# A two-layer convolution block on one core: the last image's depthwise filter is spread over more engines and its gate is placed later

## The chip, the cores and the metric

The kernel runs on one core of one Trainium2 chip. The core has five engines that run their own instruction streams in order and meet through semaphores: TensorE (PE; its weight loads are shown apart as PEld), VectorE (DVE), ScalarE (ACT), GpSimd (POOL) and SyncE (SP), which here only issues DMAs. The metric is the device time in microseconds (us) of one execution. Before the change three runs took 3316.29, 3316.36 and 3316.74 us; their median is 3316.36.

## The reference

Eight images of 384 channels and 64 x 64 points pass two residual layers. The first normalises over groups of channels, projects to queries, keys and values (1x1 convolutions), turns queries and keys by a rotary embedding, and applies linear attention in six heads. The second is the one that matters here:

```python
# layer 1, on the group-normalised x; hid = 384, P = 8
t = einsum('bchw,oc->bohw', x, w_in)                 # 1x1 expansion
tf = rfft2(t in patches of 8 x 8) * fft_filter        # filter in the frequency domain
t = irfft2(tf)                                        # back to points
t = conv3x3(t, w_dw, feature_group_count=hid)         # depthwise: 9 taps for each channel
x1, x2 = t[:, :192], t[:, 192:]
x = x + einsum('bchw,oc->bohw', gelu(x1) * x2, w_out) # gate, contraction, residual
```

Everything is 32-bit floating point.

## The kernel before

An image is cut into 8 bands of 8 rows (512 points), and its 384 channels into three tiles of 128 partitions. The channels of layer 1 are permuted so that tile 0 holds the first 128 channels of `x1`, tile 1 their partners of `x2`, and tile 2 the remaining 64 of each, in its lower and upper 64 partitions.

Layer 1 of a band runs through these steps; the names are those of the code and the trace:

1. `normalised` (L374, ACT): three instructions write `hf`, the normalised band, one band ahead.
2. `expand_filter` (L746): 12 matmuls `pi` (L752, PE), each shown as two records, give the expansion in four PSUM tiles; ACT copies each to `ht` (L759). Then 8 matmuls `pd` (L766) transform it, and four VectorE multiplies `tf` (L774) apply the frequency filter.
3. `back_transform` (L777): 48 small matmuls `pb` (L787) go back to points; six ACT copies (L797) lay the band, with a border, into one of two buffers, `ring`, which serve bands in turn. Two more ACT copies exchange border rows with the neighbour band: L802 gives this band its upper border row, L803 gives the band before its lower one. Until L803 has run, the band before lacks the row for its last three taps.
4. `first_taps` (L840): for each tile ACT writes the first of the nine taps into `dw`, in SBUF (L844). `taps` (L857): the other eight follow as VectorE instructions `acc = ring * w + acc` (L855), 24 for a band. They run one band late.
5. `gate_taps` (L863): ACT's gelu of the first part (L867) and a VectorE multiply by the second (L868) into `gated`, and the same for the two halves of tile 2 (L871, L872). There is one `gated` tile.
6. `contraction` (L878): 12 matmuls `pw` (L888 and L899) from `gated` into four PSUM tiles; ACT copies them into `y` (L913), and GpSimd's queue issues a DMA that adds `y` to the output in memory (L918), where the residual was stored before. For the very last band VectorE adds the residual itself (L915) and SP stores (L916).

For all images but the last this layer is interleaved with the key and value projections of the next image, so that TensorE always has other work. The last image has none. In its last two bands the taps of tile 2 are therefore matmuls with diagonal matrices (L822, tile `ptap`), nine for a band, on diagonals that `make_diagonals` (L813) writes once with nine ACT instructions.

PSUM has eight tiles, given out by one pool. The order of instructions on each engine is made by a scheduler when the program is built: it follows the order of the source as priority, but moves an instruction ahead of others that it expects to wait. The loop of the last image is written in the order expansion, store, normalisation of the next band, back transform, first taps, contraction of the band two before, taps and gate of the band before.

Of the kernel before, what the change touches and what calls it, by code (L numbers as in the profile page):

```python
# [9 lines left out]
F32 = mybir.dt.float32  # L10
BF16 = mybir.dt.bfloat16
AF = mybir.ActivationFunctionType
ALU = mybir.AluOpType

P = 128
C = 384
CT = 3
H = W = 64
N = H * W
NBAND = 8  # L20
BT = N // NBAND
# [96 lines left out]
def conv_blocks_kernel(ctx: ExitStack, tc: tile.TileContext, a: dict, out: bass.AP, nb: int):  # L118
    nc = tc.nc
# [4 lines left out]
    taps_pool = ctx.enter_context(tc.tile_pool(name="taps", bufs=2))  # L124
    qp = ctx.enter_context(tc.tile_pool(name="qp", bufs=2))
    small = ctx.enter_context(tc.tile_pool(name="small", bufs=2))
# [3 lines left out]
    def ps_tile(name):  # L130
        return psum.tile([P, 512], F32, tag="ps", name=name)

    def w_tile(shape, name):
        return work.tile(shape, F32, tag="w", name=name)
# [13 lines left out]
    def store_x(b, j):  # L148

        if (b, j) != (nb - 1, NBAND - 1):  # L150
            nc.sync.dma_start(x_out[b][:, :, j * BT : (j + 1) * BT], xt.pop((b, j)))
# [81 lines left out]
    def const_tile(shape, name, src, queue=nc.scalar):  # L233
        t = const.tile(shape, F32, tag=name, name=name)
        queue.dma_start(t, src)
        return t
# [8 lines left out]
    ident = groups[:, 2 * CT * NG :]  # L245
# [5 lines left out]
    scale = HD ** -0.5  # L251
# [9 lines left out]
    ring = []  # L261
# [283 lines left out]
    latest = {}  # L545
# [200 lines left out]
    def expand_filter(b, j, h, done):  # L746
        ht = w_tile([P, 4, C], f"ht_{b}_{j}")
        tf = w_tile([P, 4, C], f"tf_{b}_{j}")
        for i in range(4):
            p_ = ps_tile(f"pi_{b}_{j}_{i}")  # L750
            for t in range(CT):
                nc.tensor.matmul(  # L752
                    p_[:, :C],
                    h[:, t, i * P : (i + 1) * P],
                    w_in[:, t, :],
                    start=(t == 0),
                    stop=(t == CT - 1),
                )
            nc.scalar.copy(ht[:, i, :], p_[:, :C])  # L759
        yield  # L760

        for s in range(2):
            p_ = [ps_tile(f"pd_{b}_{j}_{2 * s + i}") for i in range(2)]
            for above in range(2):
                for i in range(2):
                    nc.tensor.matmul(  # L766
                        p_[i][halves[above], :C],
                        dft[halves[i], :],
                        ht[halves[i], 2 * s + above, :],
                        start=True,  # L770
                        stop=True,
                    )
            for i in range(2):
                nc.vector.tensor_mul(tf[:, 2 * s + i, :], p_[i][:, :C], filt)  # L774
        done.append(tf)

    def back_transform(b, j, tf):  # L777
        t = ring[j % 2]
        for m0, m1 in ((0, 2), (2, 3)):


            ps = [ps_tile(f"pb_{b}_{j}_{m0}_{u}").rearrange("p (m s i n) -> p m s i n", m=2, s=2, i=2) for u in range(2)]
            for m in range(m0, m1):
                for k in range(4):
                    for c in range(2):
                        for u, half in enumerate(halves):
                            nc.tensor.matmul(  # L787
                                ps[u][halves[c], m - m0, k // 2, k % 2],
                                tf[half, k, m * P + 64 * c : m * P + 64 * c + 64],
                                idft[half, :],  # L790
                                start=True,
                                stop=True,
                            )
            for m in range(m0, m1):
                rows = t[:, m, 1:9, 1 : W + 1].rearrange("p r (s u i c) -> p u r s i c", s=2, u=2, i=2)
                for u in range(2):
                    nc.scalar.copy(rows[:, u], ps[u][:, m - m0].rearrange("p s i (r c) -> p r s i c", r=8))  # L797
        if j == 0:
            nc.gpsimd.memset(t[:, :, 0, :], 0.0)
        else:  # L800
            before = ring[(j - 1) % 2]
            nc.scalar.copy(t[:, :, 0, :], before[:, :, 8, :])  # L802
            nc.scalar.copy(before[:, :, 9, :], t[:, :, 1, :])  # L803
        if j == NBAND - 1:
            nc.gpsimd.memset(t[:, :, 9, :], 0.0)

    dw, dw_pe, diagonals = {}, {}, []

    def on_array(b, j):

        return b == nb - 1 and j >= NBAND - 2

    def make_diagonals():  # L813
        t = small.tile([P, CT, C], F32, tag="wk", name="diagonals", bufs=1).rearrange("p t c -> p (t c)")
        for k in range(9):
            nc.scalar.activation(t[:, k * P : (k + 1) * P], ident, AF.Copy, scale=w_dw[:, 2, k : k + 1])
        diagonals.append(t)

    def array_taps(b, j, ks):

        for k in ks:
            nc.tensor.matmul(  # L822
                dw_pe[b, j].rearrange("p (r w) -> p r w", w=W),
                diagonals[0][:, k * P : (k + 1) * P],
                ring[j % 2][:, 2, k // 3 : k // 3 + 8, k % 3 : k % 3 + W],
                start=(k == 0),
                stop=(k == 8),
            )

    first_on_vector = {}  # L830

# [8 lines left out]
    def first_taps(b, j):  # L840

        acc = dw[b, j] = taps_pool.tile([P, CT, 8, W], F32, tag="dw", name=f"dw_{b}_{j}")
        for m in range(CT - on_array(b, j)):
            nc.scalar.activation(acc[:, m], ring[j % 2][:, m, 0:8, 0:W], AF.Copy, scale=w_dw[:, m, 0:1])  # L844
        if on_array(b, j):
            dw_pe[b, j] = ps_tile(f"ptap_{b}_{j}")
            array_taps(b, j, range(9 if j == NBAND - 1 else 6))

    def tile_taps(b, j, m, weights, ks=None):

        t, acc = ring[j % 2], dw[b, j]
        for k in ks or range(first_on_vector.pop((b, j, m), 1), 9):
            src = t[:, m, k // 3 : k // 3 + 8, k % 3 : k % 3 + W]
            wd = weights[:, m, k : k + 1]
            nc.vector.scalar_tensor_tensor(acc[:, m], src, wd, acc[:, m], ALU.mult, ALU.add)  # L855

    def taps(b, j):  # L857
        if on_array(b, j) and j < NBAND - 1:
            array_taps(b, j, range(6, 9))
        for m in range(CT - on_array(b, j)):  # L860
            tile_taps(b, j, m, w_dw)

    def gate_taps(b, j):  # L863
        g = gated
        af = dw.pop((b, j)).rearrange("p t r w -> p t (r w)")
        last = dw_pe.pop((b, j)) if on_array(b, j) else af[:, 2, :]
        nc.scalar.activation(g[:, :BT], af[:, 0, :], AF.Gelu)  # L867
        nc.vector.tensor_mul(g[:, :BT], g[:, :BT], af[:, 1, :])  # L868
        for h, gelu in enumerate((gelu2[64:P, :], g[64:P, BT:])):
            of = slice(h * HT, (h + 1) * HT)  # L870
            nc.scalar.activation(gelu, last[0:64, of], AF.Gelu)  # L871
            nc.vector.tensor_mul(g[halves[h], BT:], gelu, last[64:P, of])  # L872

    def depthwise_gate(b, j):
        taps(b, j)
        gate_taps(b, j)
# [43 lines left out]
    def contract(b, j):  # L920
        run(contraction(b, j))
# [29 lines left out]
    def run(*chains):  # L951

        chains = list(chains)
        while chains:
            chains = [c for c in chains if next(c, chains) is not chains]
# [139 lines left out]
    for c0, at, n in QRUNS:  # L1095

        t, p0, quarter, first = at // P, at % P, c0 // QC, c0 % QC
# [13 lines left out]
    w_dw = const_tile([P, CT, 9], "w_dw", a["w_dw"], nc.sync)  # L1111
# [55 lines left out]
    before_last, late = nothing, iter(())  # L1167
    for b in range(nb):
# [4 lines left out]
        last = b == nb - 1  # L1173
# [14 lines left out]
        for j in range(NBAND):  # L1188
# [4 lines left out]
            tf = []  # L1193
            h = normalised(b, j, params, (8, 8), "f") if j else ahead
            store_x(b, j)
            if 1 <= j < NBAND - 1:
                load_x(b + 1, j + 1)
            layer1 = expand_filter(b, j, h, tf)
            items = 1 if j < 2 else 2

# [7 lines left out]
            some(2 * items)  # L1208
            back_transform(b, j, tf[0])
            first_taps(b, j)  # L1210
            some(items)
            if j > 1:
# [11 lines left out]
        late = last_band(b)  # L1224


    make_diagonals()
    b = nb - 1
    h = ahead
    for j in range(NBAND):  # L1230
        tf = []
        layer1 = expand_filter(b, j, h, tf)
        run(layer1)
        store_x(b, j)
        if j < NBAND - 1:
            h = normalised(b, j + 1, params, (8, 8), "f")
        back_transform(b, j, tf[0])
        first_taps(b, j)
        if j >= 2:
            contract(b, j - 2)  # L1240
        if j >= 1:
            taps(b, j - 1)
            gate_taps(b, j - 1)
    contract(b, NBAND - 2)
    taps(b, NBAND - 1)
    gate_taps(b, NBAND - 1)
    contract(b, NBAND - 1)


# [39 lines left out]
```

## Time and profile before

| what | us |
|---|---|
| median of three runs | 3316.36 |
| the profiled execution, its own time | 3317.55 |
| its span, first to last instruction | 3315.8 |
| TensorE busy in the span | 3256.2 |
| VectorE busy | 2755.8 |
| ScalarE busy | 2020.4 |
| GpSimd busy | 173.7 |
| last image's layer 1, from its first `pi` (3136.58) to the end of the span | 179.2 |

Times inside the profile are counted from the start of the span. A group's line names the source line, the engine, the operation, what it writes and reads, its shape and count; then its busy time, the mean of one in ns, and the idle time of the engine just before such instructions with what ended it. A timeline row gives start and length, merged over instructions that follow each other, and in brackets the idle time before it. In a table of stretches each engine's busy time stands with its number of instructions, and then the mean clock granted to TensorE, where 1.00 is full speed.

### The profile page before, as it was taken

What the parts mean: (1) busy time and instruction counts of PE and PEld (TensorE: products, weight loads), DVE (VectorE), ACT (ScalarE), POOL (GpSimd) and SP (SyncE); (2) the same over time, 40 slices, a digit from 0 to 9 for tenths busy, and PEclk for the clock granted to TensorE, in tenths of its full rate; (3) what the DMA queues carried; (4) which work ended last, traced back from release to release, by engine and by line L of the source; (5) the groups of instructions that cost most, each with busy time, mean ns of one, the idle gap of its engine ahead of it and who ended that gap; (6) DMA issues with size and microseconds to landing.
All of it is one profiled execution on the core that took longest, in us unless ns stands there. A gap on an engine that the chain in (4) does not pass through costs nothing.

```text
span 3315.8 us, 53150 instructions
## 1 busy us (share of the span) xinstructions
PE 3256.2 (98%) x21133; PEld 1829.5 (55%) x21133; DVE 2755.8 (83%) x4528; ACT 2020.4 (61%) x4029; POOL 173.7 (5%) x321
## 2 busy tenths in 40 slices
PE   8999999999999999999999999999999999999988
PEld 5544666456664566545665456654566446664454
DVE  6577789978889688896889968998788987889697
ACT  4445666666766566755666656656576665556553
POOL 0000000100010000100001000010000100000000
PEclk9999999999999999999999999999999999999999
DMA  7324334462444523534335433445343551334112
GB/s 217 114 87 117 93 80 117 127 143 68 106 108 127 143 68 96 128 114 127 87 87 137 119 112 77 111 127 118 99 102 91 144 128 52 73 73 126 58 30 48
DMA packets 154446, 346.33 MB, mean 104 GB/s; under 512 B 29813, under 2 KB 41061, under 8 KB 146005
## 3 DMA queue, kind: packets, MB, share of 16 engines
q1 hardware_dynamic: 124500, 282.65, 27.0%
q0 software_dynamic: 29504, 60.06, 12.4%
q8 instruction: 166, 2.72, 0.3%
q14 instruction: 84, 0.68, 0.1%
q10 hardware_dynamic: 192, 0.21, 0.0%
HBM read 235.62 MB, written 99.93 MB: 101 GB/s over the span
## 4 chain that ended last, share of the span: by engine, by line
PE 90%; DVE 5%; ACT 3%; DMA 1%; issue 1%; SPq 0%; DVEq 0%; ACTq 0%
PE pf L734 15%; PE pk L491 14%; PE pi L752 14%; PE pv L507 13%; PE pq L655 13%; PE pw L888 5%; PE pb L787 3%; PE pw L899 3%; PE acc L523 3%; PE pd L766 3%; PE acc L536 2%; DVE dw L855 2%; PE pn L693 1%; ACT mt L570 1%; PE prb L717 1%
## 5 line engine op out<-in xcount | busy, mean ns | idle before, releaser
L855 DVE SCALAR_TENSOR_TENSOR dw<-ring,w_dw,dw 128x512 f32<-128x512 f32 x1401 | 977.5, 746 | 239.9 <-ACT ring L803 200.8
L491 PE MATMUL pk<-wk,x 128*128 128x384 f32 x1536 | 544.9, 496 | 0.0
L655 PE MATMUL pq<-x,wq 128*128 128x512 f32 x1152 | 521.5, 601 | 2.6 <-ACT mt L570 2.6
L752 PE MATMUL pi<-w_in,hf 128*128 128x384 f32 x1536 | 513.5, 491 | 1.3 <-ACT hf L374 1.3
L734 PE MATMUL pf<-qc,mt 128*128 128x512 f32 x1152 | 510.7, 597 | 0.0
L507 PE MATMUL pv<-wv,x 128*128 128x384 f32 x1344 | 470.0, 488 | 0.0
L491 PEld LDWEIGHTS pk<-wk,x 128*128 128x128 f32 x1536 | 283.5, 191 | 205.4 <-issue 32.5
L752 PEld LDWEIGHTS pi<-w_in,hf 128*128 128x128 f32 x1536 | 288.1, 190 | 195.8 <-issue 2.5
L514 ACT COPY v<-pv 128x384 f32<-128x384 f32 x224 | 108.7, 485 | 424.5 <-PE pv L507 423.2
L734 PEld LDWEIGHTS pf<-qc,mt 128*128 128x128 f32 x1152 | 214.3, 190 | 255.5 <-issue 239.6
L507 PEld LDWEIGHTS pv<-wv,x 128*128 128x128 f32 x1344 | 253.6, 190 | 181.4 <-issue 8.4
L655 PEld LDWEIGHTS pq<-x,wq 128*128 128x128 f32 x1152 | 212.8, 190 | 250.6 <-issue 226.2
L738 DVE SCALAR_TENSOR_TENSOR x<-pf,bfc,x 128x512 f32<-128x512 f32 x192 | 138.6, 744 | 81.9 <-PE pf L734 81.4
L379 ACT ACTIVATE qs<-qc 128x512 f32<-128x512 f32 (+1 forms) x128 | 107.0, 836 | 144.2 <-DVE qc L684 143.8
L180 ACT ACTIVATE differences<-x,shift 128x512 f32<-128x512 f32 x168 | 120.0, 714 | 103.8 <-DVE x L738 103.6
L888 PE MATMUL pw<-gated,w_out 128*128 128x256 f32 x768 | 179.3, 383 | 0.0
L494 DVE TENSOR_TENSOR kc<-pk,kvbias 128x384 f32<-128x384 f32 x256 | 140.7, 550 | 40.3 <-PE pk L491 40.2
L759 ACT COPY ht<-pi 128x384 f32<-128x384 f32 x256 | 115.1, 482 | 85.6 <-PE pi L752 81.8
L888 PEld LDWEIGHTS pw<-gated,w_out 128*128 128x128 f32 x768 | 146.7, 192 | 36.9 <-issue 6.9
L918 POOL DMA_DIRECT2D out_dram<-y x63 | 80.5, 1277 | 1544.6 <-DVE dw L855 799.1
L379 ACT ACTIVATE ks<-kc 128x1536 f32<-128x1536 f32 x64 | 95.0, 1485 | 95.1 <-DVE kc L498 94.8
L374 ACT ACTIVATE hf<-x,nb,rs 128x512 f32<-128x512 f32 x192 | 146.4, 808 | 2.4 <-DVE nb L319 2.3
(209 smaller groups left out, 4375.1 us busy)
## 6 DMA issues: line engine op xcount, KB each, us to landing
tq<-in_tq SPq DMA_DIRECT2D x64, 1024.0 KB, 4.9
x<-in_x SPq DMA_DIRECT2D x64, 768.0 KB, 6.1
tk<-in_tk SPq DMA_DIRECT2D x64, 768.0 KB, 4.5
out_dram<-x SPq DMA_DIRECT2D x63, 768.0 KB, 3.7
out_dram<-y POOLq DMA_DIRECT2D x63, 768.0 KB, 7.7
xs<-in_x SPq DMA_DIRECT2D x56, 768.0 KB, 5.9
dw<-tap POOLq DMA_DIRECT2D x14, 512.0 KB, 9.3
wk<-in_wk SPq DMA_DIRECT2D x8, 576.0 KB, 3.9
```

Of the source, the lines that this page charges most:

```text
L180: nc.scalar.activation(out[:, m, :], x_[:, m, :], AF.Identity, bias=shift[:, m : m + 1], accum_out=of_m[0])
L374: nc.scalar.activation(dst, src, AF.Identity, bias=nb_[:, t : t + 1], scale=rs[:, t : t + 1])
L379: nc.scalar.activation(e, x_, AF.Relu, scale=-1.0)
L491: nc.tensor.matmul(pk[:, :C], tokens(t), wks[:, t, :], start=(t == 0), stop=(t == CT - 1))
L494: nc.vector.tensor_add(kc[:, i, :], pk[:, :C], bias)
L507: nc.tensor.matmul(pv[:, :C], xt[b, j][:, t, i * P : (i + 1) * P], wvs[:, t, :], start=(t == 0), stop=(t == CT - 1),)
L655: nc.tensor.matmul(p_, wqs[:, t, m * P : (m + 1) * P], xt[b, j][:, t, :], start=(t == 0), stop=(t == CT - 1),)
L734: nc.tensor.matmul(p_, mt[:, t, m * P : (m + 1) * P], q[:, t, :], start=(t == 0), stop=(t == CT - 1))
L738: latest["sum"] = nc.vector.scalar_tensor_tensor(xm, p_, bfc[:, m : m + 1], xm, ALU.add, ALU.add).ins
L752: nc.tensor.matmul(p_[:, :C], h[:, t, i * P : (i + 1) * P], w_in[:, t, :], start=(t == 0), stop=(t == CT - 1),)
L855: nc.vector.scalar_tensor_tensor(acc[:, m], src, wd, acc[:, m], ALU.mult, ALU.add)
L888: nc.tensor.matmul(p_[h][:, m - m0, :], w_out[:, 0, m * P : (m + 1) * P], gated[:, h * HT : (h + 1) * HT], start=(m == m0), stop=False,)
```

## The change

Only the last image's layer 1 is touched.

- The sums of tiles 0 and 1 are kept in PSUM tiles (`sums`), where ACT writes the first tap and VectorE adds the others. The sum of tile 2 stays in SBUF.
- Tile 2's taps of bands 0 to 5 leave VectorE: ACT writes the products of three taps (`products`), GpSimd those of two early ones, and GpSimd adds all eight to the sum (`apart_taps`). In band 6 tile 2, and in band 7 tiles 1 and 2, are done by matmuls with diagonals; a second set of diagonals is made, in the buffer of the query weights.
- The taps are split by the rows they read: taps 1 to 5 (`early_taps`) are written in the band's own iteration, taps 6 to 8 (`late`), which need the row from the band below, in the next one.
- The gate of a band is written two iterations later, behind the expansion's matmuls of that iteration; `issue_after` keeps its instructions on ACT behind the third `ht` copy. The contraction of that band now stands ahead of the back transform.

In the built program nothing moves ahead of the last image's layer 1, but for the nine new ACT instructions that make the second diagonals. GpSimd's queue gets one instruction of its own ahead of its first product, which reloads its library.

```diff
+            turned = nc.scalar.copy(ht[:, i, :], p_[:, :C])
+            if i == 2:
+                latest["turned"] = turned.ins
...
     def make_diagonals():
+        for m, tag in ((2, "wk"), (1, "wq")):
+            t = small.tile([P, CT, C], F32, tag=tag, name=f"diagonals_{m}", bufs=1).rearrange("p t c -> p (t c)")
+            for k in range(9):
+                nc.scalar.activation(t[:, k * P : (k + 1) * P], ident, AF.Copy, scale=w_dw[:, m, k : k + 1])
+            diagonals[m] = t
...
+    on_array = {NBAND - 2: (2,), NBAND - 1: (1, 2)}
+    def array_taps(j, m, ks):
+        for k in ks:
+            nc.tensor.matmul(
+                sums[j][m],
+                diagonals[m][:, k * P : (k + 1) * P],
+                ring[j % 2][:, m, k // 3 : k // 3 + 8, k % 3 : k % 3 + W],
+                start=(k == 0),
+                stop=(k == 8),
+            )
+    def apart_taps(j, m, ks):
+        products = w_tile([P, CT, 8, W], f"products_{j}_{ks[0]}")
+        for i, k in enumerate(ks):
+            if i == CT:
+                products = w_tile([P, CT, 8, W], f"products_{j}_{k}")
+            product = products[:, i % CT]
+            src = ring[j % 2][:, m, k // 3 : k // 3 + 8, k % 3 : k % 3 + W]
+            wd = w_dw[:, m, k : k + 1]
+            if i < CT:
+                nc.scalar.activation(product, src, AF.Copy, scale=wd)
+            else:
+                nc.gpsimd.tensor_scalar_mul(product, src, wd)
+            nc.gpsimd.tensor_add(sums[j][m], sums[j][m], product)
+    def early_taps(j):
+        on = on_array.get(j, ())
+        sums[j] = []
+        for m in range(CT):
+            if m < 2 or m in on:
+                t = ps_tile(f"sums_{j}_{m}").rearrange("p (r w) -> p r w", w=W)
+            else:
+                t = taps_pool.tile([P, CT, 8, W], F32, tag="dw", name=f"sums_{j}_{m}")[:, m]
+            sums[j].append(t)
+            if m not in on:
+                nc.scalar.activation(t, ring[j % 2][:, m, 0:8, 0:W], AF.Copy, scale=w_dw[:, m, 0:1])
+        more_taps(j, range(1, 6))
+    def more_taps(j, ks):
+        for m in reversed(range(CT)):
+            if m in on_array.get(j, ()):
+                array_taps(j, m, range(0 if ks[0] == 1 else ks[0], ks[-1] + 1))
+            elif m == 2:
+                apart_taps(j, m, ks)
+            else:
+                for k in ks:
+                    src = ring[j % 2][:, m, k // 3 : k // 3 + 8, k % 3 : k % 3 + W]
+                    t = sums[j][m]
+                    nc.vector.scalar_tensor_tensor(t, src, w_dw[:, m, k : k + 1], t, ALU.mult, ALU.add)
...
     make_diagonals()
     b = nb - 1
     h = ahead
+    late = range(6, 9)
     for j in range(NBAND):
         tf = []
         layer1 = expand_filter(b, j, h, tf)
+        next(layer1)
+        if j >= 2:
+            with tc.issue_after(latest["turned"]):
+                gate_sums(j - 2)
         run(layer1)
         store_x(b, j)
         if j < NBAND - 1:
             h = normalised(b, j + 1, params, (8, 8), "f")
-        back_transform(b, j, tf[0])
-        first_taps(b, j)
         if j >= 2:
             contract(b, j - 2)
-        if j >= 1:
-            taps(b, j - 1)
-            gate_taps(b, j - 1)
-    contract(b, NBAND - 2)
-    taps(b, NBAND - 1)
-    gate_taps(b, NBAND - 1)
-    contract(b, NBAND - 1)
+        back_transform(b, j, tf[0])
+        if j:
+            more_taps(j - 1, late)
+        early_taps(j)
+    more_taps(NBAND - 1, late)
+    for j in (NBAND - 2, NBAND - 1):
+        gate_sums(j)
+        contract(b, j)
```

In the order that the scheduler made of it, VectorE's stream of a middle band is: the six late taps of the band before, the ten early taps of this band, the three gate multiplies, the four `tf` multiplies of the next band; and TensorE's is `pi`, `pd`, `pw`, `pb`.

## The prediction

> **What bounds the kernel now.** The page of the profile first: TensorE is busy nearly the whole span, at full clock but for the ends, so over the whole kernel only matmuls count, and a faster VectorE is worth nothing there. The change touches only the last image's filter stage, so I read that stage alone, cut at the start of each band's expansion (PE L752).
>
> ```profile
> PE 3256.2 (98%) x21133; PEld 1829.5 (55%) x21133; DVE 2755.8 (83%) x4528; ACT 2020.4 (61%) x4029; POOL 173.7 (5%) x321
> L855 DVE SCALAR_TENSOR_TENSOR dw<-ring,w_dw,dw 128x512 f32<-128x512 f32 x1401 | 977.5, 746 | 239.9 <-ACT ring L803 200.8
> ```
>
> Stretches (columns: length, busy PE, PEld, DVE, ACT, POOL, clock, DMA share, GB/s):
>
> ```profile
> 3163.72:3181.97 18.25, 16.09 (x164) 10.18 (x161) 17.14 (x29) 14.75 (x34) 0.00 (x0) 1.00 0.00 1
> 3181.97:3202.81 20.84, 17.26 (x162) 11.17 (x160) 20.75 (x34) 10.10 (x25) 1.29 (x1) 0.92 0.26 39
> 3202.81:3222.54 19.73, 17.22 (x162) 11.46 (x161) 19.64 (x32) 12.03 (x28) 1.27 (x1) 0.91 0.28 42
> 3222.54:3242.77 20.23, 17.76 (x162) 11.14 (x160) 19.93 (x33) 10.09 (x25) 1.27 (x1) 0.92 0.27 40
> ...
> 3284.55:3307.19 22.64, 22.64 (x94) 14.15 (x95) 17.75 (x29) 7.13 (x16) 2.54 (x2) 1.00 0.27 38
> ```
>
> Bands 3 to 5 are bound by VectorE (20.75 of 20.84 us busy); TensorE has some 3 us to spare and runs part of each band at a lower clock; ScalarE is half idle and GpSimd nearly empty. The last rows are TensorE's alone. The timeline of one band gives durations and hops:
>
> ```profile
> 3210.75 1.52 PE L766 MATMUL pd<-ht,dft 64*64 64x384 f32 x16
> 3214.15 1.95 DVE L774 TENSOR_TENSOR tf<-pd,filt 128x384 f32<-128x384 f32 x4
> 3214.77 3.17 PE L787 MATMUL pb<-idft,tf 64*64 64x64 f32 x96 [2.50 <-DVE tf L774]
> 3217.56 1.78 ACT L797 COPY ring<-pb 128x256 f32<-128x256 f32 x6 [2.66 <-PE pb L787]
> 3219.17 0.41 ACT L802 COPY ring<-ring 128x198 f32<-128x198 f32 x1
> 3219.42 0.41 ACT L803 COPY ring<-ring 128x198 f32<-128x198 f32 x1
> 3219.68 1.99 ACT L844 ACTIVATE dw<-ring,w_dw 128x512 f32<-128x512 f32 x3
> ...
> 3299.04 2.75 PE L888 MATMUL pw<-gated,w_out 128*128 128x256 f32 x12
> 3301.72 1.57 PE L899 MATMUL pw<-gated,w_out 64*128 64x256 f32 x12
> 3303.23 2.86 PE L888 MATMUL pw<-gated,w_out 128*128 128x256 f32 x12
> ```
>
> Call R(j) the end of copy L803 in band j, when the taps of band j-1 can be finished: here 3219.83 for j=4. Read so, R(1) to R(7) stand at 3165.76, 3179.84, 3201.67, 3219.83, 3241.63, 3259.31, 3284.55. R(1) to R(6) take 93.5 us.
>
> **The change, part by part.**
>
> *Taps taken from VectorE.* 176 taps stood there (6 bands x 24, two x 16); 120 remain (7 x 16 + 8). A tap is issued every (12.01-0.747)/17 = 0.662 us, so 37 us leave VectorE. That is not the gain, as the next wait decides.
>
> *The gate's place; the sum.* In the new order VectorE runs, per band from 2 on: 6 late taps of band j-1, 10 early taps of band j, the gate of j-1, then the four tf multiplies of j+1. TensorE runs pi, pd, pw, then pb; before, pb followed tf and pw was slipped in around it. So a ring closes: the taps need R(j); the gate stands behind all 16; pw behind the gate; pb behind pw; the ring copies behind pb; and they make R(j+1). What waits behind each: on ScalarE the last ht copy and the next normalisation behind the gelus, on VectorE tf behind the gate, on TensorE pb behind pw. The copies of y, moved ahead of the ring copies on ScalarE, start 1.16 us after pw's second half (3294.86 to 3296.02), last 1.5, and are done at R+16.7, before pb's first copy at R+17.05. Its length: 16 x 0.662 = 10.6; gate multiply 0.69 and hop 0.05 (3302.49 + 0.69 to 3303.23); pw 2.68 + 1.49 = 4.17 (3299.04, 3301.72, 3303.2); pb of two tiles with its latency 1.5 (0.9 us for 48 of 64 records, 0.25 to the copy); copies 1.61 + 0.25 + 0.41 = 2.27; hops 0.02. Sum 19.3 us, against 93.5/5 = 18.7 now: VectorE is idle for some 5 us of it, and nothing is won. Only the first step wins: in band 1 tf waits for 10 taps instead of 12, as pd + 0.98 (band 0: 3146.29 to 3147.27) gives 3159.28 and the taps 3152.54 + 6.6 = 3159.2, against 3160.62: R(1) = 3164.45. R(6) = 3164.45 + 5 x 19.3 = 3260.95.
>
> *The clock.* The trace has half-clock spells of 3.41 us, each behind a stretch of the same length with little matmul work:
>
> ```profile
> 3211.87:3215.28 3.41, 0.90 (x24) 0.36 (x16) 3.32 (x8) 2.94 (x5) 0.00 (x0) 1.00 0.07 13
> 3215.28:3218.69 3.41, 3.41 (x86) 3.20 (x87) 3.41 (x7) 1.13 (x5) 0.00 (x0) 0.50 0.02 5
> 3232.35:3235.76 3.41, 1.29 (x48) 1.02 (x48) 3.38 (x7) 1.77 (x4) 0.00 (x0) 1.00 0.00 0
> 3235.76:3239.17 3.41, 3.41 (x60) 2.46 (x55) 3.35 (x7) 0.47 (x1) 0.00 (x0) 0.50 0.02 5
> ```
>
> In the new band pi ends at R+6.7, ht's last copy, behind nine ScalarE products and the gelus, at R+8.1, pd at R+9.05, and pw waits until R+11.35. On the same grid (194.80, 215.28, 235.76, 256.24 after 3000) the stretches before it hold about 0.9, 0.9, 1.15 and 1.2 us of matmuls for bands 3 to 6: all slow, as the rows above. pw then runs 3.1, 2.7, 2.55 and 2.45 us at half speed, losing half: 5.4 us in four bands. Band 2 (2.1 and 1.9 us of 3.41) I take as undisturbed. Bounds: 0 and 5 x 1.7 = 8.5. R(6) = 3266.35. The Trainium skill's "TensorE: Matmul & The Clock Gate" (Part 1) states a free-running window of about 3.4 us and half rate after an idle one. The trace agrees, and it speaks against this change; by a gate that opened at once the time would be the sum without 5.4.
>
> *Band 7 and the tail.* R(6) to R(7): six array taps 6 x 0.857 + 0.12 (nine took 7.83, 3284.35 to 3292.18, their weight loads 0.43 apart, two to a tap) from R-0.2, pi 7.94, pd 1.55, pw 4.17, pb and a bank 1.6, copies 2.27: 22.5, against 25.25 (there the taps ran at half clock, 7.4). After R(7) TensorE has 9 + 9 + 3 = 21 array taps instead of 12, since the second tile joins: 18.1 us; pw(6) 4.19; from the last pw to the span's end 12.57 as before (3303.23 to 3315.8). With the 0.2 of early start: 34.7, against 31.25. VectorE's cover (14 taps, 9.3 us) is not the bound there.
>
> *ScalarE.* Nine products and first taps per band in place of three: 9 x 0.62 = 5.6 us (three in 1.99, 0.755 long). They delay ht to R+8.1; pd still ends 2.3 us before the gate. Cover gone, each us counts once. Nine more diagonals (0.42 long, 0.34 apart) go among ACT's waits at 3091 to 3094 (0.74, 0.50, 1.89 idle): 0, at most 1.0.
>
> *GpSimd.* Per band two products, eight adds, and the issue of y's DMA, 1.27, which stands in its queue between them. Memsets give 1747 ns for 1980 elements and 263 for 198, so 0.833 ns an element: 0.53 us for 512. An add moves three such streams, 1.38; a product two, 0.95 (estimates; bounds 0.53 and double). 14.2 us of 19.3: hidden; the late adds end near R+5.4, the gelu wants them at R+7. It becomes the bound above about 1.9 us an add. "GPSIMD Engine Reference" (3.1) has 4497 ns for an add of 2048, so about 1.1 us here as an estimate; the sum would be the same.
>
> A library reload enters GpSimd's queue in band 0. No row has one; between a ScalarE table load, 1.28, and the longest DMA landing, 12.6. It has 8 us of slack; I take 0, at most 4.
>
> *Sums in PSUM.* No row shows VectorE writing PSUM. Taps reading PSUM (L667) are 0.66 apart, the same. Bounds: 0.60 (two-input multiplies, L682) and 0.747 (no overlap): on 80 taps of the ring -5.0 to +6.8. I take 0, as by the nearest row.
>
> *Shared work of VectorE and GpSimd.* The gelu multiplies now run beside adds. Two waits of 1.38 against 1.8 of slack: 0, at most 5 in all.
>
> SP's queue keeps its order.
>
> **Sum.** 3266.35 + 22.5 + 34.7 = 3323.55, 7.8 above the span 3315.8. The profiled execution took 3317.55, 1.75 more than its span and 1.2 above the median 3316.36. On the median: 3324.
>
> **Rivals.**
> 1. *The clock stays up*: 5.4 less, 3318.7. For: waits of 2.3 us, and band 2 with 2.15 stayed at 1.00. Against: 2.3 us fell twice.
> 2. *GpSimd becomes the bound*, by slow adds, the reload or the shared work. Five bands at 1 to 3 us: 3329 to 3339. Against: 5 us free per band.
> 3. *PSUM taps are longer*: 0.70 to 0.747 gives 3327 to 3331.
> 4. *Faster*: PSUM taps turn round at once. The ring has 80; to get below 3309.7 from 3324 they must come every 0.48, or 0.55 with the clock up as a shorter ring leaves it. 512 elements beside the fixed part of 0.14 speak against.
> 5. *Nothing moves*: VectorE bound as now; excluded by the issue order, unless 56 taps less just pay the tail: 3316 to 3319, part of the first.
>
> **How the numbers follow.** Forecast 0.44 (3321.5 to 3327), rival 1 and 5 0.24, rival 2 0.14, rival 3 0.12, rival 4 0.06. Range: 0.1 out on each side, 3316.5 to 3334. About 0.2% (6.6 us) is what a measurement of this kernel tells from no change, so slower begins at 3323: of the forecast 0.37, all of 2 and 3, 0.02 of 1: 0.65. Faster 0.06, same 0.29.
>
> **What would show it.** Stretches of about 19 to 21 us between expansions with VectorE near 14 busy and about 5 idle on "ring L805"; pw waiting for the gate multiply; clock 0.5 at pw; 21 array taps ahead of the last two pw. Wrong if tap spacing in PSUM is off 0.66, if the gelus wait for GpSimd's sums, or if pb runs without waiting for pw.

## The result and the profile after

The changed kernel took 3327.40 us (median of 7 runs, 3325.32 to 3329.36) where the kernel before took 3316.74 in the same comparison: a ratio of 1.0032, 95% interval 1.0020 to 1.0044. It is slower by 0.3%; 3324 was predicted, with a range of 3316.5 to 3334. The profiled execution is the slowest of the seven: 3329.36 us, span 3327.6, where the sum had 3323.55.

The page of the changed kernel, busy time of each engine:

```profile
PE 3263.2 (98%) x21151; PEld 1829.4 (55%) x21151; DVE 2727.4 (82%) x4472; ACT 2041.3 (61%) x4073; POOL 254.1 (8%) x381
```

VectorE has 28 us less to do than before (2755.8) and GpSimd 80 more, as planned, and the time went up. Rows from the timeline of one ring (start, length, engine, line, then in brackets the idle time before), from R(2), the end of the first copy shown, to R(3), the end of the last:

```profile
3185.85 0.41 ACT L805 COPY ring<-ring 128x198 f32<-128x198 f32 x1
3186.30 10.63 DVE L914 SCALAR_TENSOR_TENSOR sums<-ring,w_dw,sums 128x512 f32<-128x512 f32 x16 [4.76 <-ACT ring L805]
3194.67 6.77 POOL L887 TENSOR_TENSOR sums<-sums,products 128x512 f32<-128x512 f32 x5
3194.68 0.86 PE L768 MATMUL pd<-ht,dft 64*64 64x384 f32 x4 [0.24 <-ACT ht L759]
3196.84 0.68 DVE L850 TENSOR_TENSOR gated<-gated,sums 128x512 f32<-128x512 f32 x1
3197.55 1.35 DVE L854 TENSOR_TENSOR gated<-gelu,sums 64x256 f32<-64x256 f32 x1
3197.57 1.99 PE L933 MATMUL pw<-gated,w_out 128*128 128x256 f32 x8 [2.03 <-DVE gated L850]
3198.93 1.38 DVE L854 TENSOR_TENSOR gated<-gated,sums 64x256 f32<-64x256 f32 x1
3200.35 1.95 DVE L776 TENSOR_TENSOR tf<-pd,filt 128x384 f32<-128x384 f32 x4
3200.96 1.16 PE L933 MATMUL pw<-gated,w_out 128*128 128x256 f32 x4 [1.39 <-DVE tf L776]
3202.05 1.57 PE L944 MATMUL pw<-gated,w_out 64*128 64x256 f32 x12
3203.55 1.63 PE L789 MATMUL pb<-idft,tf 64*64 64x64 f32 x96
...
3206.61 0.41 ACT L805 COPY ring<-ring 128x198 f32<-128x198 f32 x1
```

The ring is the predicted one: 16 taps, gate, `pw`, `pb`, copies. Its taps take 10.63, as forecast, and VectorE idles 4.76 of it. New are the two gelu multiplies L854. The same line takes 0.42 in every earlier image; here, beside GpSimd's adds (POOL L887), it takes 1.35 and 1.38. The multiply L850, which has one operand in PSUM, keeps its 0.68 beside the same adds. The `tf` multiplies stand behind the two, and the last four `pw` records wait 1.39 for `tf`: `pw` needs a PSUM tile that `pd` filled and `tf` frees. So the ring is 20.76 us long, not 19.3. R(1) to R(7) stand at 3165.48, 3186.26, 3207.02, 3230.01, 3250.77, 3270.60 and 3293.00: three rings of 20.8, one of 22.99, one of 19.83, in which the first of the two multiplies takes 0.42, and the last of 22.4.

The waits of the changed kernel from 3150 to 3300 (total, times, longest) say the same:

```profile
DVE sums L914 <- ACT ring L805: 35.9, 7, 7.0
PE pw L933 <- DVE gated L850: 9.6, 5, 2.0
PE pw L933 <- DVE tf L776: 5.5, 5, 1.4
```

The one long ring is the clock. Stretches of 3.41 us on its grid (length, busy PE, PEld, DVE, ACT, POOL, then the clock):

```profile
3216.19:3219.60 3.41, 1.39 (x8) 1.14 (x7) 3.38 (x5) 1.33 (x2) 3.17 (x4) 1.00 0.00 0
3219.60:3223.01 3.41, 2.60 (x7) 1.61 (x6) 3.35 (x6) 0.00 (x0) 2.54 (x2) 0.50 0.00 0
3223.01:3226.42 3.41, 3.41 (x14) 1.93 (x13) 0.06 (x1) 0.58 (x2) 0.00 (x0) 0.50 0.00 0
```

Two half-speed stretches, 2.2 us lost (22.99 against 20.77), and no other inside the rings. Behind R(7) TensorE's array taps set the pace:

```profile
3292.80 18.29 PE L866 MATMUL sums<-ring,diagonals 128*128 128x512 f32 x42 [1.65 <-ACT ring L804]
...
3310.93 2.75 PE L933 MATMUL pw<-gated,w_out 128*128 128x256 f32 x12
```

### The profile page after: what moved, and what is told of

It reads as the page before. It is cut to its first block, busy times and chain, and to the rows that moved or that the text cites. A ratio compares the mean times of both kernels' runs of the same rounds, so it can differ in the third digit from the quotient of the medians.

```text
span 3327.6 us, 53292 instructions
## 1 busy us (share of the span) xinstructions
PE 3263.2 (98%) x21151; PEld 1829.4 (55%) x21151; DVE 2727.4 (82%) x4472; ACT 2041.3 (61%) x4073; POOL 254.1 (8%) x381
## 4 chain that ended last, share of the span: by engine, by line
PE 90%; DVE 5%; ACT 3%; DMA 1%; issue 1%; SPq 0%; DVEq 0%; ACTq 0%
PE pf L734 15%; PE pk L491 14%; PE pi L752 14%; PE pv L507 13%; PE pq L655 13%; PE pw L933 5%; PE pb L789 3%; PE pw L944 3%; PE acc L523 3%; PE pd L768 3%; PE acc L536 2%; DVE sums L914 2%; PE pn L693 1%; ACT mt L570 1%; PE sums L866 1%
## 5 line engine op out<-in xcount | busy, mean ns | idle before, releaser
L840 DVE SCALAR_TENSOR_TENSOR dw<-ring,w_dw,dw 128x512 f32<-128x512 f32 x1225 | 858.7, 747 | 231.8 <-ACT ring L805 196.4
```

## The experiments

All runs below are compared with the kernel before on the same chip. "The ring" is the time from one R to the next.

**The early adds left out.**

```diff
+            if ks[0] != 1:
-            nc.gpsimd.tensor_add(sums[j][m], sums[j][m], product)
+                nc.gpsimd.tensor_add(sums[j][m], sums[j][m], product)
```

> GpSimd's five early adds of the third tile (taps 1 to 5) are left out in each band, so the third tile's sums are wrong; its late adds and its products stay. In the trace of the changed kernel the two gelu multiplies of 64x256 (L854) take 1.35 and 1.38 us where they take 0.42 in the kernel before, the tf multiplies stand behind them, and pw's second half waits 1.39 us for tf.
> Theory (VectorE's multiplies of two SBUF operands are slowed by GpSimd's adds beside them): without adds there the multiplies take 0.42 again, tf starts 1.9 us sooner, the wait of pw for tf goes, and the ring from copy to copy falls from 20.8 to about 19.3 us; five rings, 7 us: about 3320.
> Rival (pw's second half waits for its PSUM tile anyway, whatever the multiplies take): the multiplies fall to 0.42, but the ring stays within 0.3 of 20.8 and the time within 2 us of 3327.
> Rival (the multiplies are long because of where their operands lie): they stay at 1.35.

Measured: 3324.79 us (10 runs), ratio 1.0023 (1.0014 to 1.0032). Rows of the timeline at the same place, and two pairs of stretches on its clock grid:

```profile
3196.11 0.68 DVE L850 TENSOR_TENSOR gated<-gated,sums 128x512 f32<-128x512 f32 x1
3196.83 0.42 DVE L854 TENSOR_TENSOR gated<-gelu,sums 64x256 f32<-64x256 f32 x1
3196.85 4.37 PE L934 MATMUL pw<-gated,w_out 128*128 128x256 f32 x12 [2.03 <-DVE gated L850]
3197.28 0.42 DVE L854 TENSOR_TENSOR gated<-gated,sums 64x256 f32<-64x256 f32 x1
3197.73 1.95 DVE L776 TENSOR_TENSOR tf<-pd,filt 128x384 f32<-128x384 f32 x4
```

```profile
3193.13:3196.54 3.41, 1.45 (x8) 0.20 (x4) 3.41 (x6) 2.87 (x5) 0.79 (x1) 1.00 0.02 5
3196.54:3199.95 3.41, 3.10 (x7) 2.50 (x8) 3.05 (x7) 0.00 (x0) 0.00 (x0) 0.50 0.00 0
3213.61:3217.02 3.41, 1.55 (x12) 0.21 (x6) 3.41 (x6) 2.98 (x6) 0.88 (x1) 1.00 0.01 2
3217.02:3220.43 3.41, 3.00 (x7) 2.46 (x8) 3.15 (x7) 0.00 (x0) 0.00 (x0) 0.50 0.00 0
```

The multiplies are back at 0.42, so the adds beside them are what makes them long, and the place of the operands alone does not; and `pw` runs its twelve records without the break at `tf`. Yet the rings take 20.68, 20.59, 20.53, 20.50 and 19.07. By its number the first rival nearly holds (four rings within 0.3 of 20.8, and 3324.79 where it said 2 us around 3327); by its mechanism it doesn't, since that wait is gone. What came instead is a half-speed spell over `pw` in each of the four long rings: twelve records in 4.37 us.

**TensorE kept busy while it waits**, on top of that.

```diff
+            again = 3 if b == nb - 1 and s and 2 <= j < NBAND - 1 else 1
-            for above in range(2):
+            for above in again * list(range(2)):
```

> On top of leaving the early adds out: in bands 2 to 6 the matmuls pd of the second pair are issued three times over, with the same result each time, about 2 us of TensorE's work in the 2.0 us in which it otherwise waits for the gate multiply; no instruction waits longer for it, as the gate ends last.
> In the run without early adds the multiplies were back at 0.42 us and pw's wait for tf was gone, but four rings took 20.5 to 20.7 us in place of 19.3, and in each a spell of half clock lay over pw (12 records in 4.37 us for 2.75).
> Theory (the spells follow TensorE's wait, and cost 1.2 us a ring): the spells go, the rings fall to 19.1 to 19.4, four of them 5 us: about 3320.
> Rival (the rings' extra length has another cause, or the spells come at any rate): rings stay at 20.5, time within 1.5 us of 3325.

Measured: 3319.26 us (10 runs), ratio 1.0007 (0.9997 to 1.0016). Timeline:

```profile
3193.52 2.15 PE L769 MATMUL pd<-ht,dft 64*64 64x384 f32 x20 [0.25 <-ACT ht L759]
...
3196.39 2.86 PE L935 MATMUL pw<-gated,w_out 128*128 128x256 f32 x12 [0.72 <-DVE gated L851]
```

The repeated records lengthen the second part of `pd` from 0.86 to 2.15, and the wait before `pw` falls from 2.03 to 0.72. No spell is left in the rings, and all five take 19.06 or 19.07. So the spells follow TensorE's wait, cost 6.0 us in the run before (82.30 less 4 x 19.07), and the bare ring is 19.07 long. With the slow multiplies and the spells both gone, the time can't be told from that of the kernel before (the interval holds 1): with its rings bare the change wins nothing and loses nothing.

**The same filler with all the adds in.** The edit is the second one alone.

> The changed kernel with all its work, and the matmuls pd of the second pair three times over in bands 2 to 6, as in the run that did so without the early adds. Theory (in the changed kernel the slow multiplies, and not the clock, make the rings 20.8 long; the clock takes part only in a run's odd spell, 2.2 us in one ring of the profile): rings of 20.7 to 20.8 and one of 19.8 all the same, no spell in them, and a time at the low end of the changed kernel's runs, 3325 to 3327. Rival (a clock loss is hidden in every ring): the rings fall to 20 or less, 3322 or less.

Measured: 3325.93 us (7 runs, 3325.51 to 3328.36), ratio 1.0029 (1.0018 to 1.0041). The profile has no half-speed stretch behind its first `pi`; its rings take 20.80, 20.78, 20.76, 20.80 and 19.82, and its timeline still has the break:

```profile
3196.06 1.38 DVE L855 TENSOR_TENSOR gated<-gelu,sums 64x256 f32<-64x256 f32 x1
...
3199.49 1.16 PE L934 MATMUL pw<-gated,w_out 128*128 128x256 f32 x4 [1.42 <-DVE tf L777]
```

In the changed kernel it is the slow multiplies that make the ring 20.8, 1.7 over the bare one, and the clock takes part only in the odd spell. Either of the two costs alone gives about the same ring, which is why taking away one gained little.

**The sums of tiles 0 and 1 in SBUF.**

```diff
+        acc = taps_pool.tile([P, CT, 8, W], F32, tag="dw", name=f"sums_{j}")
-            if m < 2 or m in on:
+            if m in on:
...
-                t = taps_pool.tile([P, CT, 8, W], F32, tag="dw", name=f"sums_{j}_{m}")[:, m]
+                t = acc[:, m]
```

> The sums of the first two tiles stand in SBUF, as in the kernel before, in place of PSUM; all else as changed. Theory (an instruction of VectorE with two large SBUF operands is slowed while GpSimd works): the taps, 0.66 us apart with one operand in PSUM, lengthen while GpSimd runs, which is 13 to 14 of 20.8 us in a band; if they lengthen by the 0.9 us that the gelu multiplies did, a band's 16 taps take 20 us or more in place of 10.6, and the time is 3355 or more. Rival (the place of the sums plays no part, taps are 0.66 apart in the kernel before too): spacing 0.66, time within 3 us of 3327.

Measured: 3381.82 us (4 runs), ratio 1.0194 (1.0179 to 1.0209). A row of its timeline, and two of its groups in the last image's stage:

```profile
3200.20 19.72 DVE L915 SCALAR_TENSOR_TENSOR sums<-ring,w_dw,sums 128x512 f32<-128x512 f32 x16 [7.48 <-ACT ring L805]
```

```profile
L915 DVE SCALAR_TENSOR_TENSOR sums<-ring,w_dw,sums 128x512 f32<-128x512 f32 x120 | 134.5, 1189 | 49.8 <-ACT ring L805 46.2 <-ACT sums L901 3.3
L887 POOL TENSOR_TENSOR sums<-sums,products 128x512 f32<-128x512 f32 x48 | 73.9, 1539 | 20.5 <-ACT products L884 17.8
```

Sixteen taps take 19.72 in place of 10.63 and the rings 30.7: of the 9.9 us that a ring grew, 9.1 are the taps, and most of the rest is `pw`, whose twelve 128x256 records run at half clock, in 5.39. GpSimd's adds take 1.54 in place of 1.28 (61.7 us for 48 in the changed kernel). In the kernel before the same taps, with both operands in SBUF, stood 0.66 apart with GpSimd idle. The two engines hold each other up, and in these runs only where both of VectorE's large operands lie in SBUF. Beside a row of adds they take turns, one tap to one add, and a pair takes 1.67 us; the 1.23 that a tap takes on average is a mean over stretches with adds, with products and with an idle GpSimd. The Trainium skill gives a reason in "SBUF — State Buffer" (SBUF: two separate sides): the two share a pair of SBUF ports under an exclusive lock, taken for a whole instruction, and a VectorE instruction with two SBUF inputs needs it against a GpSimd instruction that reads SBUF. The runs agree on who is held up: a multiply goes from 0.42 to 1.38, a tap from 0.66 to 1.67 beside adds, and a tap whose sum lies in PSUM stays at 0.66. They agree less on the length: 1.67 for a pair is under the 1.94 that a tap and an add would take one behind the other (0.66 and 1.28), so some part of the two overlaps. The sums in PSUM are worth 54 us to the changed kernel.

**The last band's second tile back on VectorE.**

```diff
-    on_array = {NBAND - 2: (2,), NBAND - 1: (1, 2)}
+    on_array = {NBAND - 2: (2,), NBAND - 1: (2,)}
```

> The last band's second tile goes back from TensorE to VectorE; all else as changed. Theory (the tail after the last border copy is TensorE's 21 array taps, 18.3 us, with pw behind them): nine array taps, 7.8 us, leave TensorE; VectorE then has 22 taps, 14.6 us, and the gate of band 6 between them, and becomes the bound at some 17 to 18 us where TensorE stood at 22.4 before its last pw: 3 to 4.5 us less, about 3323.5. Rival (VectorE has no room, since its gate multiplies wait and stand in order): within 1 us of 3327.

Measured: 3326.78 us (7 runs), ratio 1.0029 (1.0018 to 1.0040): no change that can be told from 3327.40, a miss. Behind R(7), 3289.97, its timeline has:

```profile
3290.00 14.58 DVE L914 SCALAR_TENSOR_TENSOR sums<-ring,w_dw,sums 128x512 f32<-128x512 f32 x22 [6.65 <-ACT ring L805]
3290.02 10.57 PE L866 MATMUL sums<-ring,diagonals 128*128 128x512 f32 x24 [1.89 <-ACT ring L805]
...
3304.49 0.68 DVE L850 TENSOR_TENSOR gated<-gated,sums 128x512 f32<-128x512 f32 x1
...
3305.32 4.51 PE L933 MATMUL pw<-gated,w_out 128*128 128x256 f32 x12 [4.73 <-DVE gated L850]
```

The gate of band 6 was queued behind all 22 taps, so the rival holds by its number and its reason. TensorE was done with its array taps at 3300.6, waited 4.73 us, and then ran `pw` at half speed. The array taps were not the only bound; the order on VectorE was one just behind them. From R(7) to the end it took 33.73 us in place of 34.60.

**The gate early.** The gate of band j-1 is written right behind band j's first two early taps; the other eight are held back behind the next `tf`.

```diff
...
-        more_taps(j, range(1, 6))
+        more_taps(j, range(1, 6), (2,))
+        more_taps(j, range(1, 2), (1, 0))
...
-        layer1 = expand_filter(b, j, h, tf)
-        next(layer1)
-        if j >= 2:
-            with tc.issue_after(latest["turned"]):
-                gate_sums(j - 2)
-        run(layer1)
+        run(expand_filter(b, j, h, tf))
+        if j:
+            with tc.issue_after(latest["tf"]):
+                more_taps(j - 1, range(2, 6), (1, 0))
...
         early_taps(j)
+        if j:
+            gate_sums(j - 1)
...
```

> The gate of band j-1 stands directly behind that band's late taps and two of band j's early taps, no longer behind all 16; the other eight early taps are held back behind the next tf. All work stays. Theory (the ring taps, gate, pw, pb, copies sets the pace): the gate leaves the ring; VectorE finishes its multiplies about 9 us after the border copy, when pd ends, pw (4.2) follows pd directly, then pb (1.5) and the copies (2.3): 16.7 to 17 us from copy to copy in place of 20.8, for four of the rings and part of a fifth, and the tail a little shorter: 3307 to 3312. Rival (VectorE's and ScalarE's order gives the gain back: gelus wait for taps, ht for gelus): rings of 19 to 20 us, 3319 to 3324. Rival (GpSimd, busy 15 us a band, is the bound): its wait stands ahead of the gelus of the third tile.

Measured: 3308.86 us (10 runs), ratio 0.9977 (0.9967 to 0.9987), faster than the kernel before. The rings from R(2) to R(6) take 16.98 to 16.99; the first, where the gate still stands behind 16 taps and a half-speed spell falls, 20.14. Rows of the timeline from R(3) = 3201.37 on:

```profile
3201.40 5.36 DVE L915 SCALAR_TENSOR_TENSOR sums<-ring,w_dw,sums 128x512 f32<-128x512 f32 x8 [1.23 <-ACT ring L805]
...
3206.70 3.27 POOL L886 TENSOR_SCALAR products<-ring,w_dw 128x512 f32<-128x512 f32 x2
3207.38 0.69 DVE L850 TENSOR_TENSOR gated<-gated,sums 128x512 f32<-128x512 f32 x1 [0.62 <-ACT gated L849]
3208.10 0.42 DVE L854 TENSOR_TENSOR gated<-gelu,sums 64x256 f32<-64x256 f32 x1
3208.55 0.81 DVE L854 TENSOR_TENSOR gated<-gated,sums 64x256 f32<-64x256 f32 x1
3208.65 2.01 PE L768 MATMUL pd<-ht,dft 64*64 64x384 f32 x16 [0.55 <-ACT ht L759]
...
3210.59 2.86 PE L934 MATMUL pw<-gated,w_out 128*128 128x256 f32 x12
```

`pw` follows `pd` without a wait, VectorE waits 1.23 for the border copy in place of 4.76, and no spell falls in these four rings. All the work of the change is in this run, spread over the engines in the same way. So the order, with the gate behind the 16 taps, made the spread a loss: 18.5 us lie between the two medians. Not all of it is the ring itself. In the new place the two gelu multiplies meet GpSimd's products in place of its adds and take 0.42 and 0.81, so most of their delay goes as well. From R(1) to R(6) this run takes 88.08 us, the changed kernel 105.12 and five bare rings 95.35: 7.3 of the 17.0 us are against the bare ring, and 9.8 are what the slow multiplies and the clock had put on it.

**The same with less on TensorE at the end.**

```diff
-    on_array = {NBAND - 2: (2,), NBAND - 1: (1, 2)}
+    on_array = {NBAND - 1: (2,)}
```

> On top of the early gate: band 6 has its third tile filtered by ScalarE and GpSimd like the bands before, and the last band's second tile goes back to VectorE, so TensorE has nine array taps in all in place of 27.
> Theory (from R(6) on, TensorE's array taps set the pace: 22.4 us to R(7) against 17.0 in the bands before): the ring to R(7) falls to 17, 5.4 us; behind R(7) VectorE's 22 taps, 14.6, and the multiplies between them end about where TensorE's taps and pw(6) did: 32 against 32.8. Sum about 3303.
> Rival (behind R(7) GpSimd's late adds for band 6 hold the gelus and so VectorE's and TensorE's order): a tail of 35 or more, 3306 or more.

Measured: 3300.02 us (4 runs), ratio 0.9950 (0.9935 to 0.9964). The ring to R(7) falls from 22.39 to 16.99, as expected; from R(7) = 3269.68 to the end it takes 28.82, 3 less than expected, and 4.0 less than the 32.82 of the early gate alone. The gain lies ahead of the last `pw`, which starts 19.08 behind R(7) in place of 23.26. A transfer has a part in the tail too, but the early gate alone already had it: the landing times of two of the last band's output stores (group, KB, us from issue to landing), first in the changed kernel, then here and in the early gate alone:

```profile
out_dram<-x SPq DMA_DIRECT2D x2, 256.0 KB, 5.3
```

```profile
out_dram<-x SPq DMA_DIRECT2D x2, 256.0 KB, 2.4
```

Band 6's `y`, 768 KB, takes 7.6 us to land in both. In the changed kernel it was issued at 3316.70, 3.1 us ahead of these stores; here at 3284.62, 8.8 ahead, so that it had landed. In all ten profiles of the case the stores take 5.2 to 5.4 where `y` is still under way and 2.4 where it has landed. From the first of these stores to the end it takes 7.8 us in the changed kernel and 4.9 in the early gate alone, more than the 1.8 by which that run's tail is shorter.

**TensorE begins the second tile of the last band and VectorE ends it**, in one PSUM tile.

```diff
+    begun_on_array = {NBAND - 1: (1,)}
...
-                stop=(k == 8),
+                stop=(k == (5 if m in begun_on_array.get(j, ()) else 8)),
...
-            if m in on_array.get(j, ()):
+            begun = m in begun_on_array.get(j, ()) and ks[0] < 6
+            if begun or m in on_array.get(j, ()):
```

> As the run before it, but in the last band TensorE begins the second tile: its first six taps are array matmuls, 5.2 us, and VectorE adds the last three on the same PSUM tile. VectorE has 17 taps behind R(7) in place of 22.
> Theory (VectorE sets the tail): 5 taps, 3.3 us, go from its path; about 3 us less than the run before it: about 3300. Rival (pw(6) and the array taps, 13.1 + 4.2 us, on TensorE set it): within 1 us of the run before it.

Measured: 3299.04 us (4 runs), ratio 0.9946 (0.9929 to 0.9963): the lowest time of the case, 0.5% under the kernel before, but 1.0 under the run before it and not 3, about as much as four runs of one kernel lie apart (0.9 and 1.8). Rows of the timeline behind R(7) = 3269.32:

```profile
3281.15 6.28 PE L867 MATMUL sums<-ring,diagonals 128*128 128x512 f32 x14
...
3284.89 2.34 DVE L917 SCALAR_TENSOR_TENSOR sums<-ring,w_dw,sums 128x512 f32<-128x512 f32 x3 [1.70 <-PE sums L867]
```

VectorE has room and waits 1.70 for TensorE's taps; `pw` of the last band starts at 18.75 behind R(7) in place of 19.08. The rival holds: TensorE's row of taps, `pw` and taps again is the bound there.

## Why the prediction was right, and where not

The direction was right, the ring that the gate closes was there as drawn, 0.2 us shorter, and the time was 3.4 us short (3324 to 3327.40), inside the range but 0.4 above the forecast's own 3321.5 to 3327. But the ring explains only why nothing was won. Against the kernel before, R(1) to R(6) take 11.6 us more (105.12 to 93.5): 1.8 by the bare rings, 2.2 by the clock, and 7.6 by a term that the prediction put at nothing. In the profile the gap of 4.05 (3327.6 less 3323.55) comes apart so:

| step of the prediction | forecast | measured | difference |
|---|---|---|---|
| start of the stage, taken from the run before | 3136.58 | 3137.81 | +1.23 |
| from there to R(1) | 27.87 | 27.67 | -0.20 |
| five bare rings | 96.5 | 95.35 | -1.15 |
| clock at `pw` | 5.4 | 2.2 | -3.2 |
| shared work of VectorE and GpSimd | 0 | 7.57 | +7.57 |
| R(6) to R(7) | 22.5 | 22.4 | -0.1 |
| R(7) to the end | 34.7 | 34.6 | -0.1 |

The bare rings are 5 x 19.07 from the runs with the filler. The shared work is the rest of the 105.12 us from R(1) to R(6): 105.12 - 95.35 - 2.2.

- *Start of the stage.* Not the change: one ScalarE table load of the unchanged first image already stood at 503.22 in place of 501.98, and over the nine other profiles of this case the first `pi` stands anywhere from 3134.67 to 3137.21. From that load to the first `pi` it is 2634.6 us in both, so the second diagonals, which lie between, cost nothing, as forecast.
- *Shared work.* This is the step that failed: "Two waits of 1.38 against 1.8 of slack: 0, at most 5 in all." The waits were smaller than it took, 0.93 to 0.97 each (1.35 to 1.39 less 0.42), and still came through: the slack was wrong. It had `tf` behind the gate, but left out that the last four of `pw`'s first twelve records need a PSUM tile from `tf`. Of 1.89 us added (2.73 less 0.84), 1.39 show as TensorE's wait at `tf`, and the ring is 1.7 longer. The total, 7.57, lies outside the bound of 5. Rival 2 counted the shared work among its causes, at 1 to 3 us a band: that part of it came true in four of five rings, though GpSimd was not the bound.
- *The clock.* The mechanism was right: without the adds the spells came in four rings and cost 6.0 (forecast 5.4, bounds 0 to 8.5). In the changed kernel the clock cost 2.2 only. That the break in `pw` moved the rings off the clock's grid (20.77 against six stretches of 3.41, 20.48) is argued, not shown. The stretch ahead of a spell need not be idle: those shown, in the prediction and here, hold 0.90 to 1.55 us of matmuls. The two errors, +7.57 and -3.2, have opposite signs, and by that luck the sum came out better than its terms.
- *Sums in PSUM.* Sixteen taps in 10.63, 0.66 apart: 0 extra, and the rivals of longer or shorter PSUM taps are out. What the prediction didn't see is that the same taps in SBUF would have cost 54 us more beside GpSimd. The sums also hold PSUM tiles of the pool from which `pw` takes its own; what that alone costs is not shown by any run.
- *GpSimd.* An add takes 1.28 (own estimate 1.38) and a product 1.56 (estimate 0.95, inside the bounds); the late adds end at R+5.4, as forecast, and nothing waits for them. The library reload has no row and delays nothing that the trace shows: the first product starts 0.28 us behind the memset before it. GpSimd was not the bound, but it was felt through VectorE.
- *ScalarE.* Nine products a band are hidden, as forecast: `pd` ends 2.0 us before `pw` starts (3195.54 and 3197.57; forecast 2.3).
- *The tail.* Both terms within 0.1. But the array taps were not worth what their length says: taking nine of them away gave back only 0.9 while the gate of band 6 stood behind VectorE's taps; with that gate early, twelve fewer gave 4.0 (32.82 to 28.82).

## What to carry to other kernels

Work taken off a busy engine gains nothing when the new order puts a late result, here the gate, behind everything that engine does: first look for the ring that the new order closes, then place the few instructions that others wait for ahead of those that nobody waits for. Before GpSimd gets work, look for VectorE instructions whose two large operands lie in SBUF and that will run beside it; one of the operands in PSUM avoids the wait. Two delays in the same ring can stand in for each other, so take both away before calling either one harmless.

## What the runs showed of the hardware

- VectorE and GpSimd: a 64x256 multiply of two SBUF operands 0.42 alone and 1.35 to 1.39 beside adds; 128x512 taps 0.66 apart alone and, with both large operands in SBUF, in turns with GpSimd's adds, 1.67 for a tap and an add; with the sum in PSUM 0.66 beside the same adds. GpSimd's adds take 1.28 beside the taps in PSUM and 1.54 beside those in SBUF, its products 1.56 and 1.87 (means).
- A product by a factor for each partition takes GpSimd longer (1.56) than an add of two tensors (1.28) of the same size.
- With the early adds gone four rings came close to six stretches of the clock's grid (20.68, 20.59, 20.53, 20.50; six are 20.48), each with its slow spell, and 1.3 us of repeated matmuls a ring, whose results change nothing, gained 5.5 us.
- The last stores of 256 KB land in 2.4 us, or in 5.2 to 5.4 where a store of 768 KB is still under way.
